# A two-layer transformer with routed experts on one core: bias in tiles on GpSimd, loads moved past returns, a count and a routing step moved, PSUM banks of the FFN reordered

## The chip, the cores and the metric

The kernel runs on one core of a Trainium2 chip. Its engines are TensorE (PE in the profile, PEld for its weight loads), VectorE (DVE), ScalarE (ACT), GpSimd (POOL) and SyncE (SP), which issues most transfers (DMA). The metric is the device time of one execution in microseconds (us); lower is better.

## The reference

Eight batches of 512 tokens by 512 features (fp32) pass through two layers. After each of the four blocks comes a layer norm over the features of block input plus block output.

```python
x = ln(x + attn0(x))   # 16 heads of 32, causal softmax, biases on q, k, v and the output
x = ln(x + ffn0(x))    # router: softmax over 8 experts, top 2; gated SiLU experts (512 -> 256 -> 512), with LoRA
x = ln(x + attn1(x))   # RMS-normed input, 8 query heads in 2 groups of 64, no mask, inner residual
x = ln(x + ffn1(x))    # 1408 hidden, integer weights minus 128, scaled by row, gated SiLU
```

## The kernel before

One program runs four stages, and TensorE is never meant to stop between them. A planner orders each engine's instructions when the program is built, from its own estimate of when each is ready; inside `in_order` the named engines keep the order of the source instead. Engines then run their lists in order and wait on semaphores. `tc.issue_after(i)` queues what is traced in it behind instruction i on i's engine, with no wait for i to finish; `add_manual_dep` with NoSync does the same for one pair on one engine.

*Attention of layer 0* (`attention0`, 0 to about 690 us). Eight batches b, four groups g of four heads, three units u of key tiles (`UNITS`: tile 0; tiles 1 and 3; tile 2). A unit computes scores (`scores`, PSUM tile sc), an exponential on ACT (L1476), a causal select on POOL for each key tile (`affine_select`, L1486), and, one unit later, the product with the values (`product`, av, L1503) and the sums on DVE (L1511). `normalise` takes the row sums (rs), a reciprocal (L1521), the product into aoT (L1522), and on POOL adds the inverses to g_total (L1077). The lists `todo[g, u]` hang other work between: q, k and v of this and the next batch, the output projection of the batch before (`project`, ps_o), its transposition, its router logits (`score`), and for the batch before that `choose` (top 2), `dispatch` (ranks) and `enter` (one-hot products into ps_table, read on DVE at L601 to L603). Batches 0 to 5 are transposed through DRAM (`Turn`: DVE blocks, four writes of 256 KB, one read back of 1 MB, L106), batches 6 and 7 by TensorE (`turn`, ps_x1T, L1427). The small PSUM tiles ps_q, ps_k, ps_o, ps_table, ps_count, ps_x1T and others take turns in the two banks of the pool "mm". Beside it POOL merges the LoRA deltas into the expert weights (L814, L823). In the loop over groups, g = 2 loads the next xT and adds the output bias to x on POOL (L1595, one instruction for the batch); g = 3 loads the next x. In the last batch `soon` counts the tokens of each expert (ps_count, L613 to L615) and takes the first rows to gather.

*Experts* (`Tiles`, to about 1061 us). Tiles of 128 tokens of one expert: gathered by POOL (`fetch`, L873, up to ten tiles ahead), transposed on DVE (`blocks`, L904), sent to DRAM and read back (pair, xrT), multiplied (`half` or `gate_up`, ps_gu), then `down` (ps_y), and written to results. One `step` does the half of tile i + 2 and the down of tile i. The first steps stand between the projection, turn, choose, dispatch and enter of the last batch. The tiles from number 16 on use tokens that `fixed` takes after the last enter.

*Attention of layer 1* (`Attention1`, to about 1607 us), all compute engines in order: `prepare` gathers two results a token (L722), adds and norms them, transposes through DRAM (`blocks`) or TensorE (`turn`). The rows of batches 2 to 7 (x, 1 MB each, L1969) are loaded ahead of it.

*FFN of layer 1* (`IntegerFfn`, to the end): `hidden` (ps_g, ps_u, L1222; ACT L1225; DVE L1227; then hT in a high and a low part) and `out` (ps_f, L1238). The last batch ends tile by tile in `last_rows`. PSUM has eight banks: in attention of layer 1 they go to "mm" (2), scores (2 tiles of 2 banks), av (2); the FFN pools d_gu (g and u, two each) and d_o (four) take all eight again.

Of the kernel before, what the change touches and what calls it, by code (L numbers as in the profile page):

```python
# [82 lines left out]
class Turn:  # L83
# [21 lines left out]
    def back(self, room):  # L105
        self.nc.sync.dma_start(out=room, in_=self.dram.rearrange("p k i f -> p (k i f)"))  # L106

# [319 lines left out]
class Router:  # L427
# [4 lines left out]
    def __init__(self, env, keep, pool, small, tmp, dram):  # L432
# [38 lines left out]
        nc.gpsimd.iota(i, pattern=[[0, 1]], base=0, channel_multiplier=1)  # L471
        lane = pool.tile([P, 1], F32, name="r_lane")
        nc.vector.tensor_copy(lane, i)
        self.signed = pool.tile([P, NT], F32, name="r_signed")
        for t in range(NT):
            nc.vector.tensor_scalar(self.signed[:, t : t + 1], lane, float(P * t - GAP + (P * t >= GAP)), None, ALU.add)
        i = tmp.tile([P, S], F32, tag="r_inv", name="r_columns_i", bufs=2)[:, : E * E_TILES].bitcast(I32)
        nc.gpsimd.iota(i, pattern=[[1, E * E_TILES]], base=0, channel_multiplier=0)
# [117 lines left out]
    def enter(self, ps, b, token, column, held, columns):  # L596

        nc, n = self.nc, TOP_K * NT
        for i in range(n):
            matmul_by_columns(nc, ps, token[:, i, :], column[:, i, :], i == 0, i == n - 1, columns)  # L600
        nc.vector.tensor_scalar(held, ps, 0.0, float((S + 1) * b + GAP), ALU.not_equal, ALU.mult)  # L601
        nc.vector.tensor_tensor(self.table, ps, self.table, ALU.add)
        nc.vector.tensor_tensor(self.table, held, self.table, ALU.add)  # L603

    def row_at(self, b, t):

        return (S + 1) * b + P * t + (P * t >= GAP)

    def soon(self, pool, ps, held):


        nc, half = self.nc, E // 2
        nc.tensor.matmul(ps, lhsT=self.ones, rhs=self.carry, start=True, stop=True)  # L613
        nc.vector.tensor_reduce(held, ps[:, :half], AX.X, ALU.min)
        nc.vector.tensor_scalar(held, held, float(SOON * P), None, ALU.is_ge)  # L615
        tokens = pool.tile([P, half, SOON], I32, name="t_soon")
        nc.vector.tensor_copy(tokens, self.by_expert()[:, :half, :SOON])
        return lambda e, j: tokens[:, e, j : j + 1]
# [9 lines left out]

    def tables(self, pool, ps, held):

# [7 lines left out]
        self.tokens = tokens = pool.tile([P, N_FREE + FREE], I32, name="t_tokens")  # L638
        nc.vector.memset(tokens, 0)
        nc.tensor.matmul(ps, lhsT=self.ones, rhs=self.carry, start=True, stop=True)  # L640
        n_i = pool.tile([P, E], I32, name="t_n_i")
        nc.vector.tensor_scalar(n_i, ps, P - 1.0, None, ALU.add)
# [184 lines left out]
class Tiles:  # L827
# [184 lines left out]

    def step(self):
        i = self.next
        self.next += 1
        if i == 0:
            self.down(i)
        if i + 2 < N_FIXED:
            self.half(i + 2)
        elif N_FIXED <= i + 1 < self.n:  # L1020
            self.gate_up(i + 1, lambda: self.turn_hidden(i))
        elif i + 1 == self.n:
            self.turn_hidden(i)
        while self.fetched <= i + 10 and (self.fetched < self.n_soon or self.of_fixed is not None):
            self.fetch(self.fetched)
            self.fetched += 1
        if i:
            self.down(i)
        for n in (4, 5) if i == 0 else (5,):
            if i + n < self.BY_BLOCKS:  # L1030
                self.turn_rows(i + n)
        if i + 6 >= self.BY_BLOCKS:
            self.pair_back(i + 6)
        if i + 7 >= self.BY_BLOCKS:
            self.blocks(i + 7)
# [109 lines left out]
class IntegerFfn:  # L1145
# [45 lines left out]
    def run(self, held_out, last_norm):  # L1191
        tc, nc, weights = self.env.tc, self.nc, self.weights
        with ExitStack() as phase:
            self.work = phase.enter_context(tc.tile_pool(name="d_work", bufs=1))
            self.p_gu = phase.enter_context(tc.tile_pool(name="d_gu", bufs=2, space=PSUM, reuse_waits="tile"))
            self.p_o = phase.enter_context(tc.tile_pool(name="d_o", bufs=1, space=PSUM, reuse_waits="tile"))
            weights.open(phase.enter_context(tc.tile_pool(name="d_weights", bufs=1)), 3 * NHID - weights.at)
            self.sd = self.work.tile([P, D], F32, name="sd")
            with tc.tile_pool(name="d_slots", bufs=1) as slots:
                while weights.at < 3 * NHID:  # L1200
                    weights.load(slots, 4, 3 * NHID)
                    weights.convert()
                nc.sync.dma_start(out=self.sd, in_=self.env.ins.s_down.partition_broadcast(P))
            with tc.tile_pool(name="d_raw", bufs=1) as self.raw:
                for b in range(NB - 1):
                    self.batch(b)
                    if b == 0:
                        last_norm()
                        ps = self.p_gu.tile([1, 1], F32, tag="g", name="ps_held")
                        nc.scalar.dma_start(out=held_out, in_=self.guard.partitions_held(self.env.const, ps))  # L1210
            self.late = phase.enter_context(tc.tile_pool(name="d_late", bufs=self.HELD))
            self.batch(NB - 1)
# [65 lines left out]
    def last_rows(self, b, t, x):  # L1278
# [8 lines left out]
        if t == NT - 1:  # L1287
            nc.vector.tensor_scalar(x, x, mv[:, 0:1], rstd, ALU.subtract, ALU.mult)
        else:
            shift = small.tile([P, 1], F32, name="shift2")  # L1290
            nc.gpsimd.tensor_scalar(shift, mv[:, 0:1], rstd, -1.0, ALU.mult, ALU.mult)
            nc.scalar.activation(x, x, AF.Identity, bias=shift, scale=rstd)
        nc.scalar.dma_start(out=env.ins.out[b][ts(t, P), :], in_=x)


def attention0(env, guard, keep, routes, experts, dram, p_mm, tiles_ctx):
# [8 lines left out]
    with ExitStack() as phase:  # L1305
# [102 lines left out]
        by_blocks = NB - 2  # L1408
        turns = Turn(env, dram, NT, "turned0")

        def room(b):
            x1Ts[b] = work.tile([P, ND, S], F32, tag="x1T", name="x1T")

        def blocks(b):
            room(b)
            flat = x1Ts[b].rearrange("p k s -> p (k s)")
            for t in range(NT):
                turns.blocks(flat, t, xs[b][:, t, :])
            turns.out(flat)
            turns.back(flat)  # L1420

# [36 lines left out]
        def enter(rows, mm=mm, columns=HD):  # L1458
            router.enter(mm([P, E * E_TILES], "ps_table"), *rows, columns)

        def scores(b, g, u):
# [22 lines left out]
            for kt in UNITS[u]:  # L1484
                first = p[:, :, at : at + P]
                nc.gpsimd.affine_select(out=first, in_=first, pattern=[[0, 4], [1, P]], compare_op=ALU.is_ge, fill=0.0,  # L1486
                                        base=0, channel_multiplier=-1)
                at += S - P * kt
            for thunk in merging.pop(n, []):
                thunk()  # L1490
# [23 lines left out]
        def normalise(b, g, acc):  # L1514
# [6 lines left out]
            nc.vector.reciprocal(r_inv, r_inv)  # L1521
            nc.vector.tensor_tensor(aoTs[b][:, g, :], av, r_inv, ALU.mult)  # L1522
            guard.watch_inverses(r_inv)

        merging = {}

        def plan(b):
# [26 lines left out]
            if b > 1:  # L1554
                todo[0, 0].append(lambda: choose(b - 2, mm=aside))
                todo[1, 0].append(lambda: dispatch(b - 2))
                todo[1, 2].append(lambda: enter(one_hot(b - 2, range(NT))))
            if last:
# [20 lines left out]
        def soon():  # L1579
            tiles.of_soon = router.soon(routes, mm([P, E], "ps_count"), guard.routed[:, 0:1])  # L1580

# [6 lines left out]
        for b in range(NB):  # L1588
            todo, late = plan(b)
            for g in range(ND):  # L1590
                if g == 2:
                    if b + 1 < NB:
                        load_xT(b + 1)

                    nc.gpsimd.tensor_tensor(xs[b], xs[b], row[:, 1:2, :].to_broadcast([P, NT, D]), ALU.add)  # L1595
                if g == 3 and b + 1 < NB:
                    load_x(b + 1)
                if b == NB // 2 and g == 0:
# [42 lines left out]
        score(b)  # L1641
        choose(b, P)
        tiles.step()
# [8 lines left out]
        order.close()  # L1652
    return router, tiles, router.tables(routes, p_mm.tile([P, E], F32, tag="mm", name="ps_count"), guard.routed[:, 1:2])


class Attention1:
# [21 lines left out]
    def prepare(self, b):  # L1678
# [17 lines left out]
        def blocks(t):  # L1696
# [3 lines left out]
            if t == NT - 1:  # L1700
                self.turn.out(st["room"])
                st["hT"] = own.tile([P, ND, S], F32, tag="hT", name="hT1")
                self.turn.back(st["hT"].rearrange("p k s -> p (k s)"))

# [62 lines left out]
    def batches(self, work, p_sc, p_av, weights, split):  # L1767
# [171 lines left out]
        prepare_table(AF.Silu)  # L1939
        banks += [p_sc.tile([P, 2, S], F32, tag="sc", name="ps_o1")[:, 0, :] for _ in range(2)]  # L1940
        banks.append(self.mm([P, D], "ps_o1"))
# [11 lines left out]
def usual_pass(tc, ins, held_out):  # L1953
    nc = tc.nc
    with ExitStack() as ctx:
# [4 lines left out]
        with tc.tile_pool(name="a_mm", bufs=2, space=PSUM) as p_mm, ExitStack() as attn1_ctx:  # L1960
# [28 lines left out]
            env.open_stream(ctx, range(2, NB), side="right")  # L1989
            for b in range(2, NB):  # L1990
                load_rows(b)
            weights = IntegerWeights(env, guard)
# [312 lines left out]
```

## Time and profile before

| | us |
|---|---|
| three runs: median (lowest to highest) | 2108.59 (2108.27 to 2109.18) |
| profiled execution | 2106.08 |
| its span, first to last instruction | 2104.20 |
| TensorE busy in the span | 2074.4 |
| first matmul starts / last matmul ends | 4.6 / 2095.2 |

Busy time adds up what an engine's instructions took; a matmul's end is modelled. A row of waits names who waited, on whom, for how long in total, how often, and the longest. A row of the timeline has start and length in us, then engine, line, operation, out<-in, and in brackets the idle time before it with what ended it. The granted TensorE clock was 0.999 on average.

### The profile page before, as it was taken

The numbers are of one execution on the slowest core, as the hardware profiler recorded it, in microseconds if no ns is written. First come the engines' busy times: TensorE is split into PE (matmuls) and PEld (weight loads), VectorE is DVE, ScalarE is ACT, GpSimd is POOL, SyncE is SP. The second block draws the span as 40 slices with busy tenths as digits, with TensorE's granted clock in tenths as the row PEclk, the third lists the DMA queues.
The fourth block names the chain that finished last, engine by engine and source line by source line (L and its number), as shares of the span: only waits on it lengthen the run. The fifth ranks groups of instructions, "written<-read, shape, count | busy, mean of one in ns | idle before, by whom it ended". The sixth has DMA issues, their size and how long they took to land. (4 is left out here: it accounts for less than half of the span.)

```text
span 2104.2 us, 35813 instructions
## 1 busy us (share of the span) xinstructions
PE 2074.4 (99%) x15074; PEld 1048.8 (50%) x15074; DVE 1270.6 (60%) x1963; ACT 606.8 (29%) x840; POOL 496.0 (24%) x488
## 2 busy tenths in 40 slices
PE   8999999999999999999999999999999999999998
PEld 2333333333334677774433333333335888888886
DVE  2666776776768623234257898887867644555443
ACT  2333433324333111111143333333332322222222
POOL 2343534434333221222042221223101000000000
PEclk9999999999999999999999999999999999999999
DMA  9020303415222568877451322132102311111000
GB/s 326 22 65 38 101 22 110 136 52 156 85 98 102 172 199 239 251 227 209 149 206 51 100 81 71 56 95 81 41 1 71 100 41 61 60 61 60 21 21 22
DMA packets 181946, 213.39 MB, mean 101 GB/s; under 512 B 72570, under 2 KB 125818, under 8 KB 178706
## 3 DMA queue, kind: packets, MB, share of 16 engines
q1 hardware_dynamic: 170496, 175.34, 26.8%
q0 software_dynamic: 10560, 34.61, 5.6%
q8 instruction: 121, 1.98, 0.4%
q10 hardware_dynamic: 722, 1.07, 0.1%
q14 instruction: 47, 0.39, 0.1%
HBM read 132.58 MB, written 78.40 MB: 100 GB/s over the span
## 5 line engine op out<-in xcount | busy, mean ns | idle before, releaser
L1077 POOL TENSOR_TENSOR g_total<-g_total,r_inv 128x512 f32<-128x512 f32 x64 | 90.1, 1408 | 488.3 <-DVE r_inv L1862 269.9
L1476 ACT ACTIVATE p<-sc 128x2048 f32<-128x2048 f32 (+1 forms) x96 | 153.0, 1594 | 174.7 <-PE sc L65 150.7
L1511 DVE TENSOR_TENSOR p<-p 128x1536 f32<-128x1536 f32 (+2 forms) x96 | 149.5, 1557 | 77.6 <-POOL p L1486 74.4
L1227 DVE SCALAR_TENSOR_TENSOR hT<-ps_u,vec,sg 128x512 f32<-128x512 f32 x88 | 65.6, 745 | 187.2 <-PE ps_u L1222 187.1
L1238 PE MATMUL ps_f<-ffn_w,h_half 128*128 128x512 f32 x664 | 168.1, 393 | 2.6 <-DVE h_half L1233 2.0
L958 PE MATMUL ps_gu<-xrT,experts 128*128 128x256 f32 x736 | 166.7, 380 | 0.4 <-DMA xrT<-pair 0.4
L958 PEld LDWEIGHTS ps_gu<-xrT,experts 128*128 128x128 f32 x736 | 139.5, 190 | 35.6 <-issue 19.2
L1832 ACT ACTIVATE p<-sc 128x1024 f32<-128x1024 f32 x128 | 124.2, 1022 | 100.2 <-PE sc L65 91.5
L1862 DVE RECIPROCAL r_inv<-r_inv 128x512 f32<-128x512 f32 x32 | 107.1, 3346 | 67.8 <-ACT r_inv L1074 67.8
L1238 PEld LDWEIGHTS ps_f<-ffn_w,h_half 128*128 128x128 f32 x664 | 122.9, 188 | 34.6 <-DVE h_half L1233 8.0
L1222 PE MATMUL ps_g<-x_high,ffn_w 128*128 128x512 f32 x352 | 137.3, 390 | 0.9 <-DVE x L1804 0.9
L1222 PE MATMUL ps_g<-x_low,ffn_w 128*128 128x512 f32 x352 | 137.2, 390 | 0.0
L1222 PE MATMUL ps_u<-x_low,ffn_w 128*128 128x512 f32 x352 | 137.1, 390 | 0.0
L1222 PE MATMUL ps_u<-x_high,ffn_w 128*128 128x512 f32 x352 | 137.1, 389 | 0.0
L65 PE MATMUL sc<-qT,kT 64*64 64x512 f32 x1024 | 124.7, 602 | 1.2 <-ACT qT L1729 0.9
L65 PE MATMUL ps_q<-experts 128*32 128x512 f32 x1024 | 120.8, 601 | 4.9 <-DMA experts<-in_xT 4.6
L65 PE MATMUL ps_v<-experts 128*32 128x512 f32 x1024 | 120.9, 595 | 0.0
L1851 PE MATMUL av<-p,v 128*64 128x512 f32 x512 | 120.9, 594 | 0.0
L1486 POOL TENSOR_SCALAR_AFFINE_SELECT p<-p 128x512 f32<-128x512 f32 x128 | 82.7, 657 | 157.6 <-ACT p L1476 155.0
L1225 ACT ACTIVATE sg<-ps_g,vec 128x512 f32<-128x512 f32 x88 | 60.6, 689 | 199.8 <-PE ps_g L1222 199.8
L65 PE MATMUL ps_o<-attn_out,aoT 128*64 128x512 f32 x512 | 116.4, 598 | 0.0
L65 PE MATMUL ps_k<-experts 128*32 128x512 f32 x1024 | 116.3, 595 | 0.0
(278 smaller groups left out, 3248.3 us busy)
## 6 DMA issues: line engine op xcount, KB each, us to landing
results<-y SPq DMA_DIRECT2D x68, 256.0 KB, 3.2
pair<-xrT SPq DMA_DIRECT2D x30, 512.0 KB, 3.0
xrT<-pair SPq DMA_DIRECT2D x120, 128.0 KB, 3.8
turned<-turned SPq DMA_DIRECT2D x56, 256.0 KB, 4.0
x<-in_x SPq DMA_DIRECT2D x8, 1024.0 KB, 8.6
rows<-x SPq DMA_DIRECT2D x32, 256.0 KB, 2.3
x<-rows SPq DMA_DIRECT2D x16, 512.0 KB, 12.5
experts<-in_xT SPq DMA_DIRECT2D x7, 1024.0 KB, 8.5
```

Source lines behind the costliest of these rows:

```text
L65: nc.tensor.matmul(out[m], lhsT=lhsT[:, m], rhs=rhs, start=start, stop=stop)
L958: nc.tensor.matmul(ps[:, j, :], lhsT=w, rhs=xT[:, c, :], start=c == 0, stop=c == ND - 1)
L1077: self.nc.gpsimd.tensor_tensor(self.total, self.total, r_inv, ALU.add)
L1222: nc.tensor.matmul(ps, lhsT=w[:, ts(dc, P)], rhs=x[:, dc, :], start=(dc, i) == (0, 0), stop=(dc, i) == (ND - 1, 1))
L1227: nc.vector.scalar_tensor_tensor(hT, u, vec[:, V_SU + c : V_SU + c + 1], sg, ALU.mult, ALU.mult)
L1238: self.nc.tensor.matmul(os[t], lhsT=h[:, ts(t, P)], rhs=self.weights(2 * NHID + c), start=(c, i) == (0, 0), stop=(c, i) == (NHID - 1, 1))
L1476: nc.scalar.activation(p, sc[:, :, :width], AF.Exp, scale=scale)
L1486: nc.gpsimd.affine_select(out=first, in_=first, pattern=[[0, 4], [1, P]], compare_op=ALU.is_ge, fill=0.0, base=0, channel_multiplier=-1)
L1511: nc.vector.tensor_tensor(total[:, :, P * kt :], total[:, :, P * kt :], p[:, :, at : at + w], ALU.add)
L1832: nc.scalar.activation(p, sc, AF.Exp, scale=scale)
L1851: nc.tensor.matmul(st["av"][HD * j : HD * (j + 1), :], lhsT=st["v"][:, kt, HD * j : HD * (j + 1)], rhs=p[:, j, :], start=kt == 0, stop=kt ...
L1862: nc.vector.reciprocal(r_inv, r_inv)
```

## The change

1. The bias of layer 0 is no longer added for a whole batch at g = 2. Batches 1 to 6 add tile 0, tiles 1 and 2, and tile 3 behind the selects of unit 1 in groups 1, 2 and 3; batch 7 adds two tiles in group 1 and two in group 2; batch 0 keeps one add, behind the selects of group 2.
2. From batch 1 on xT of the next batch is loaded at g = 0, and x of the next batch is queued behind the read back of the turned rows (`returned`).
3. `soon` only copies the carry; the count, its minimum and its comparison go to `tables`. In the last batch the product of L1522 is queued behind `enter`'s read of the table (`behind`).
4. In the last batch `choose` goes into a step (`amid`, between its half and its down), and with this one more step stands before `dispatch` and all that follows it.
5. d_o is opened before d_gu; two output tiles of attention of layer 1 use the second half of their score buffers.
6. Only the rows of batch 2 are loaded ahead of layer 1's attention; those of batch b + 1 are queued behind the read back of batch b.
7. The last tile of the output is normed and written in two halves, from two queues.

```diff
+        self.soon_carry = pool.tile([P, half], F32, name="r_soon_carry")
+        nc.vector.tensor_copy(self.soon_carry, self.carry[:, :half])
-        nc.tensor.matmul(ps, lhsT=self.ones, rhs=self.carry, start=True, stop=True)
-        nc.vector.tensor_reduce(held, ps[:, :half], AX.X, ALU.min)
-        nc.vector.tensor_scalar(held, held, float(SOON * P), None, ALU.is_ge)
...
         nc.tensor.matmul(ps, lhsT=self.ones, rhs=self.carry, start=True, stop=True)
+        nc.tensor.matmul(soon, lhsT=self.ones, rhs=self.soon_carry, start=True, stop=True)
+        nc.vector.tensor_reduce(held_soon, soon, AX.X, ALU.min)
+        nc.vector.tensor_scalar(held_soon, held_soon, float(SOON * P), None, ALU.is_ge)
...
-    def step(self):
+    def step(self, amid=lambda: None):
...
+        amid()
         if i:
             self.down(i)
...
+            self.p_o = phase.enter_context(tc.tile_pool(name="d_o", bufs=1, space=PSUM, reuse_waits="tile"))
             self.p_gu = phase.enter_context(tc.tile_pool(name="d_gu", bufs=2, space=PSUM, reuse_waits="tile"))
-            self.p_o = phase.enter_context(tc.tile_pool(name="d_o", bufs=1, space=PSUM, reuse_waits="tile"))
...
-            nc.vector.tensor_scalar(x, x, mv[:, 0:1], rstd, ALU.subtract, ALU.mult)
+            for i, queue in enumerate((nc.sync, nc.scalar)):
+                half = x[:, ts(i, D // 2)]
+                nc.vector.tensor_scalar(half, half, mv[:, 0:1], rstd, ALU.subtract, ALU.mult)
+                queue.dma_start(out=env.ins.out[b][ts(t, P), ts(i, D // 2)], in_=half)
...
+            if u == 1 and b:
+                with tc.issue_after(select.ins):
+                    for t in ((), (0, 1), (2, 3), ())[g] if b == NB - 1 else ((), (0,), (1, 2), (3,))[g]:
+                        x = xs[b][:, t, :]
+                        nc.gpsimd.tensor_tensor(x, x, row[:, 1, :], ALU.add)
+            elif (g, u) == (2, 1):
+                with tc.issue_after(select.ins):
+                    nc.gpsimd.tensor_tensor(xs[b], xs[b], row[:, 1:2, :].to_broadcast([P, NT, D]), ALU.add)
...
-                todo[1, 2].append(lambda: enter(one_hot(b - 2, range(NT))))
+                if last:
+                    todo[1, 2].append(lambda: behind(enter(one_hot(b - 2, range(NT))), normed[0]))
+                else:
+                    todo[1, 2].append(lambda: enter(one_hot(b - 2, range(NT))))
...
-                if g == 2:
-                    if b + 1 < NB:
-                        load_xT(b + 1)
-
-                    nc.gpsimd.tensor_tensor(xs[b], xs[b], row[:, 1:2, :].to_broadcast([P, NT, D]), ALU.add)
+                if g == (0 if b else 2) and b + 1 < NB:
+                    load_xT(b + 1)
                 if g == 3 and b + 1 < NB:
-                    load_x(b + 1)
+                    with tc.issue_after(returned[0].ins) if b else ExitStack():
+                        load_x(b + 1)
...
-        choose(b, P)
+        tiles.step(lambda: choose(b, P))
         tiles.step()
         dispatch(b, tiles.bank, P)
...
-                self.turn.back(st["hT"].rearrange("p k s -> p (k s)"))
+                back = self.turn.back(st["hT"].rearrange("p k s -> p (k s)"))
+                if 2 <= b < NB - 1:
+                    with self.env.tc.issue_after(back.ins):
+                        self.load_rows(b + 1)
...
-        banks += [p_sc.tile([P, 2, S], F32, tag="sc", name="ps_o1")[:, 0, :] for _ in range(2)]
+        banks += [p_sc.tile([P, 2, S], F32, tag="sc", name="ps_o1")[:, 1, :] for _ in range(2)]
...
-            for b in range(2, NB):
-                load_rows(b)
+            load_rows(2)
+            attention.load_rows = load_rows
```

Beside these, the small tile r_lane shares a buffer with r_columns.

## The prediction

> **What bounds the kernel now.** I read the page's first part, then TensorE's own waits, then the timeline and the transfers around each wait.
>
> ```profile
> PE 2074.4 (99%) x15074; PEld 1048.8 (50%) x15074; DVE 1270.6 (60%) x1963; ACT 606.8 (29%) x840; POOL 496.0 (24%) x488
> ```
>
> TensorE is busy for 2074.4 of 2104.2 us, and the change removes no matmul, so only the other 29.8 us can be won. Its first matmul starts at 4.6 us and its last ends at 2095.2 us: 4.6 us lie ahead, 9.0 us behind, some 16.2 us between. TensorE's waits name those (what waited, on whom: total, times, longest):
>
> ```profile
> PE ps_q L65 <- DMA experts<-in_xT: 4.6, 1, 4.6
> PE ps_f L1238 <- DVE h_half L1233: 2.0, 7, 0.5
> PE av L1503 <- POOL p L1486: 1.9, 3, 1.0
> PE ps_logits L504 <- DMA x1T<-turned: 1.8, 2, 1.5
> PE ps_x1T L1427 <- DVE g_routed L614: 1.5, 1, 1.5
> PE sc L65 <- ACT p L1476: 1.2, 1, 1.2
> PE sc L65 <- ACT qT L1729: 0.9, 1, 0.9
> PE ps_g L1222 <- DVE x L1804: 0.9, 1, 0.9
> ...
> PE ps_r L65 <- ACT logits L1440: 0.8, 1, 0.8
> PE ps_rank L65 <- DVE earlier L553: 0.7, 1, 0.7
> PE ps_f L1238 <- issue: 0.6, 1, 0.6
> PE rs L1518 <- ACT first_turned L925: 0.6, 1, 0.6
> ...
> PE ps_gu L958 <- DMA xrT<-pair: 0.4, 1, 0.4
> ```
>
> Rows 3, 4, 5, 8 and the ps_r and ps_rank rows are what the edits touch: 1.9 + 1.8 + 1.5 + 0.9 + 0.8 + 0.7 = 7.6 us. All other work runs beside TensorE, so an edit counts only through such a row, or through a new one.
>
> **The change part by part.** Signs: minus is time won.
>
> *Bias on POOL, -1.9 us.* Before, one add for a whole batch:
>
> ```profile
> L1595 POOL TENSOR_TENSOR x<-x,row 128x2048 f32<-128x2048 f32 x8 | 36.5, 4560 | 9.3 <-DMA x<-in_x 3.7 <-DMA results<-g_total 3.3 <-issue 2.3
> ```
>
> The planner put it where x lands, in group 3 of the batch before. At 498.21 and 583.68 it stands ahead of two selects whose exponential ended at 497.51 and 582.57; the selects start at 502.73 and 588.19, and av waits 0.60 and 1.01 us (0.27 in the batch at 158.7). After, each piece is queued behind the select pair of unit 1. A 128x512 add on POOL took 1.27 us at best (L823 at 469.63) and 1.77 on average (L823 and L814), so 28 pieces are 36 to 50 us plus 4.56 for batch 0: up to 18 us more POOL work, on an engine busy 24%. What waits behind a piece: the add of g_total, a merge, the next select. In groups 1 and 2 the pair ended at 457.43 and POOL was idle for 10.1 us; two slow pieces (4.5 us at the 2.26 of the slower merges) fit. In group 3 the pair would end near 498.9 and the next exponential ends at 502.95: 4 us for one piece. The last batch has two pieces behind the selects that end at 656.32, and the next select is ready at 660.65; two gathers of first rows move back by 2 to 4 us, of which none feeds the two tiles turned at 669. I take the whole row; the ends are -1.9 and rival B.
>
> *Loads apart from returns, -1.8 us.* Both waits on x1T are for the 1 MB return of the transposed rows. Around the longer one, by the transfers from 400 to 420 us (KB, us to landing):
>
> ```profile
> x<-in_x SPq DMA_DIRECT2D x1, 1024.0 KB, 8.4
> x1T<-turned SPq DMA_DIRECT2D x1, 1024.0 KB, 8.6
> ```
>
> x was issued at 404.07 and landed at 412.51; the return, issued at 408.74, landed at 417.39, 4.9 us after x; TensorE wanted it at 416.07. The four writes ahead, issued from 400.10 on, landed at 408.62 with x behind them. Now x is issued behind the return, and the next xT at the start of the batch, some 60 us earlier. The Trainium skill (DMA: Bandwidth & Descriptors, "Queues, rings and completion order") says that SP's descriptors start in ring order on each DMA engine but that completion is not first in, first out. Read as order, the return needs only its 4.9 us: landing at 413.6, 2.5 us to spare, -1.8. Read as sharing, x issued 0.4 us behind takes its half again and the sum here is 0. The 4.9 us after x's landing speak for order; I take -1.8. SP's queue: six xT loads move ahead of rows, merges and turns of their batch. A merge load behind one would wait up to 8.4 us more; the loads issued at 430.02 and 431.09 are used at 445.36, 12 us after landing. x is next used by the bias, 30 us or more later. Both are costed at nothing because of these leads; without them a late merge add would hold the select behind it, as the 4.56 us add did.
>
> *The count moved, and an order edge, -1.2 us.* The timeline of the last batch (start, us):
>
> ```profile
> 647.04 0.68 DVE L1522 TENSOR_TENSOR aoT<-av,r_inv 128x512 f32<-128x512 f32 x1
> 648.24 0.41 DVE L601 TENSOR_SCALAR one_hot<-ps_table 128x256 f32<-128x256 f32 x1
> 648.58 0.41 DVE L602 TENSOR_TENSOR r_table<-ps_table,r_table 128x256 f32<-128x256 f32 x1
> 648.90 0.15 DVE L614 TENSOR_REDUCE g_routed<-ps_count 128x1 f32<-128x4 f32 x1
> 649.13 1.06 PE L1427 MATMUL ps_x1T<-ident,x 128*128 128x128 f32 x8 [1.46 <-DVE g_routed L614]
> ```
>
> The two "mm" banks go round: ps_k, ps_table, ps_count, first ps_x1T, second ps_x1T. The first ps_x1T takes ps_table's bank, read until 648.98, so dropping L614 alone would win 0.1. But without ps_count it takes ps_k's bank, read by ACT at 644.61: it starts at 647.67. The second now takes ps_table's, wanted near 648.2. The edge puts L1522 (0.68) behind L602, so that read ends near 648.3. Left: 0.1 to 0.4 of 1.46; I take -1.2. Only the release of an av bank waits for L1522, needed again about 10 us later. Added: a 128x4 copy (0.17, the row of L551); count, reduce and compare (0.3) move to the table stage, where TensorE is busy 303.56 of 304 us and DVE 93.
>
> *Routing moved, -1.5 us.* ps_r waited 0.76 for the logits copy, ps_rank 0.72 for choose's chain on DVE (724.67 to 730.91). In between now stand a half (3.6 us) before ps_r, and a down (1.9), another half and a down (5.5) before ps_rank: 7.4 against 6.2. Both rows go. But gathers of fixed rows, first at 744.21, start one step (5.3 us) later against the tiles. Their transposes already wait on DVE (2.2 and 0.8 us), without holding TensorE. The pair that came 0.44 late at 758 shared its return (8 us instead of 3 to 5) with these gathers and gains. I take -0.2 for it; ends -0.4 and +5.3 (rival C).
>
> *FFN banks, -0.6 us.* The first ps_g waits 0.85 for the last residual (1607.24 to 1607.98), which reads its bank. By the order of the pools ps_g now gets the unread half of a score buffer. Next in line is ps_f at 1616.21, 0.62 late: hT ran at 1614.71, behind two norms and a weight conversion on DVE, although its inputs were there at 1611.97. If that order stays, the 0.85 only moves into this wait: 0. If the planner puts hT first, both go: -1.5. I take -0.6.
>
> *Rows of layer 1, -0.3 us.* Twelve 512 KB loads stood beside the gathers at 1068 to 1078, which took 7.9 us each against 3.5 to 5 at 1119 to 1129. Now two do. POOL's sums start 3.6 us sooner; TensorE's small waits on that chain up to 1107 add to 0.9, of which some belongs to bank turns. Ends 0 and -0.9. The later loads, one batch at a time, have 40 us.
>
> *Last tile in halves, -0.4 us.* L1288 took 0.55, its transfer 2.5 to landing. The first half leaves 0.25 sooner, each carries half. The same page ("Rules for kernel authors") speaks against this: spreading transfers over issuing engines doesn't help, they share the same DMA engines[...]. In the trace the bytes move in about 1 us of the 2.5, so at most 0.5 and the 0.25. Between: -0.4, ends 0 and -0.6.
>
> *Restarts, -0.6 us.* A wait costs more than its idle time: at 1616.21 matmuls start 1.01 apart instead of 0.23, 0.78 for 0.62 idle. Nine waits by 0.16 are 1.4; I take 0.6, since most stand before short or column-tiled matmuls.
>
> Sum: 1.9 + 1.8 + 1.2 + 1.5 + 0.2 + 0.6 + 0.3 + 0.4 + 0.6 = 8.5. The planner reorders every engine after such edits; for new waits I give back 1.0. So -7.5 us: the profiled execution from 2106.08 (span 2104.20 plus 1.88) to 2098.6; its before stands 2.5 under the median of 2108.59, so the median goes to 2101.1.
>
> **The rivals.** *A: the waits move.* The next name in each queue takes over: hT in the FFN, the table's read, x beside the return. For: those three are within 1 us of the waits removed. Against: margins of 2.5 and 4 us elsewhere. Gain 3: 2105.6. This also holds the case that an edge changes nothing.
>
> *B: slower, through POOL's pieces.* Instead of one add a batch, 20 groups have a piece in front of the next select. If each holds av by 0.63 (the mean of the three waits), that is 12.6, against 8.5 - 1.9 - 1.0 = 5.6 of other gains: +7, 2115.6. It decides when a piece and the g_total add outlast 4 us in group 3, or 10 us in groups 1 and 2. Against: the slowest such adds took 2.3.
>
> *C: fixed rows late.* One step once, 5.3: gain 2 left, 2106.6.
>
> **How the numbers follow.** Measured runs spread by 0.04%; 0.2%, 4.2 us, is about what can be told from no change. Forecast 0.64, all faster; A 0.20 (0.02 faster, 0.16 same, 0.02 slower); C 0.05 (0.04 same, 0.01 slower); B 0.11. So 0.66, 0.20, 0.14. With every part at its better end the sum is 12: 2096.5. The forecast's own range is 2096.5 to 2104.3; to 2109 it takes in A and C, leaving out B and a tail.
>
> **What would show it.** Right: no av row on POOL L1486, no ps_logits row on x1T, under 0.4 us before ps_x1T, no ps_r and ps_rank rows, ps_g without a wait, gathers near 5 us in layer 1's first batch, TensorE busy the same 2074. Wrong: a ps_f wait grown to 1.4 us (FFN part 0); av waits in groups 1 to 3 (B); ps_gu waiting on xrT between 760 and 800 us (C); a return still landing 8 us after its issue.

## The result: 0.9% slower, and the profile after

| | before | after |
|---|---|---|
| median of six runs, us (lowest to highest) | 2108.89 (2107.06 to 2111.30) | 2127.34 (2125.17 to 2130.59) |
| profiled execution / its span, us | 2106.08 / 2104.20 | 2128.18 / 2126.2 |
| mean granted TensorE clock | 0.999 | 0.995 |

The ratio is 1.0087 (95% interval 1.0074 to 1.0100): slower by 18 us, where 7.5 us of gain were forecast, and outside the range. The page's row of TensorE and its waits after the change, in the order that they were shown of before:

```profile
PE 2081.2 (98%) x15074; PEld 1049.7 (49%) x15074; DVE 1286.7 (61%) x1965; ACT 607.2 (29%) x840; POOL 502.2 (24%) x509
```

```profile
PE ps_logits L505 <- DMA x1T<-turned: 12.3, 4, 5.5
PE av L1522 <- POOL p L1497: 5.8, 6, 1.0
PE ps_q L65 <- DMA experts<-in_xT: 4.6, 1, 4.6
PE rs L1887 <- DVE total L1868: 3.1, 1, 3.1
...
PE ps_f L1245 <- PE ps_u L1229: 0.8, 1, 0.8
PE ps_x1T L1438 <- DVE r_table L603: 0.7, 1, 0.7
PE ps_rank L65 <- DVE earlier L554: 0.7, 1, 0.7
```

Read the rows against the list that the prediction gave itself. The rows of ps_g, ps_r and ps_gu are gone, and ps_x1T halved. But the return of the turned rows, which was to vanish (1.8), became the largest wait of all; av, which was to vanish (1.9), waits 5.8; and rs, 0.2 before, waits 3.1. Up to its last matmul TensorE was idle for 35.9 us instead of 20.8: 15.1 more. And it was busy for 6.8 us more (2081.2 against 2074.4) with the same 15074 matmuls: that is the clock, worked out below. The two make the 22 us between the spans.

**The return.** SP's own timeline in batch 4 shows what stands ahead of the read back of the turned rows (start, length, queue, line). Before, and then after:

```profile
404.07 1.24 SPq L1330 DMA_DIRECT2D x<-in_x  x1
408.74 0.33 SPq L106 DMA_DIRECT2D x1T<-turned  x1
409.11 2.00 SPq L824 DMA_DIRECT2D merged<-merged  x2
411.16 1.34 SPq L1326 DMA_DIRECT2D experts<-in_xT  x1
```

```profile
414.25 2.61 SPq L830 DMA_DIRECT2D merged<-merged  x2
416.95 0.42 SPq L1336 DMA_DIRECT2D experts<-in_xT  x1
417.55 0.43 SPq L106 DMA_DIRECT2D x1T<-turned  x1
418.02 0.43 SPq L1340 DMA_DIRECT2D x<-in_x  x1
```

Now x is behind the return as the edge says, and the planner has filled the place ahead of it with xT, which is as large (1024 KB). In both lists it is the xT of two batches on (batch 6): before the change, too, the planner issued it a batch ahead of the source line that loads it. Two merged stores, which wait for POOL's merges, stand ahead as well, and the return is issued 3.5 us before TensorE wants it (417.55 for 421.06) where it was 7.3 before (408.74 for 416.07). It lands 8.9 us after its issue (8.6 before), and TensorE waits 5.5.

**The pieces.** All six av waits are alike, 0.97 us in group 3 of batches 1 to 6, behind two pieces in group 2. The groups of VectorE by form show which neighbour changed, the norm L195 of 128x512 (busy, mean ns). Before, and then after:

```profile
L195 DVE TENSOR_SCALAR x<-x,mv,rstd 128x512 f32<-128x512 f32 x60 | 33.3, 616 | 15.5 <-POOL rstd L193 15.5
```

```profile
L195 DVE TENSOR_SCALAR x<-x,mv,rstd 128x512 f32<-128x512 f32 x60 | 44.9, 810 | 15.5 <-POOL rstd L193 15.5
```

In batch 4 the two pieces and the four norms run side by side:

```profile
400.27 2.86 POOL L1504 TENSOR_TENSOR x<-x,row 128x512 f32<-128x512 f32 x2
398.96 4.46 DVE L195 TENSOR_SCALAR x<-x,mv,rstd 128x512 f32<-128x512 f32 x4 [1.48 <-POOL rstd L193]
```

The group took 11.6 us more for six batches of two pieces, which is 0.97 us of VectorE for each piece beside it. The pieces pay as well: 1.44 to 1.46 us each there, 1.27 to 1.30 elsewhere. In batch 4 the four norms took 4.46 us instead of 2.53; the transposes, the reciprocal, the g_total add on POOL and the select behind that add came later in turn, and av waited for the select.

### The profile page after: what moved, and what is told of

It reads as the page before. It is cut to its first block, busy times and chain, and to the rows that moved or that the text cites. A ratio compares the mean times of both kernels' runs of the same rounds, so it can differ in the third digit from the quotient of the medians.

```text
span 2126.2 us, 35858 instructions
## 1 busy us (share of the span) xinstructions
PE 2081.2 (98%) x15074; PEld 1049.7 (49%) x15074; DVE 1286.7 (61%) x1965; ACT 607.2 (29%) x840; POOL 502.2 (24%) x509
## 4 chain that ended last, share of the span: by engine, by line
PE 43%; DVE 4%; issue 1%; DMA 1%; POOL 1%; ACT 0%; DVEq 0%; POOLq 0%; ACTq 0%
PE ps_f L1245 6%; PE ps_u L1229 6%; PE ps_g L1229 6%; PE sc L65 5%; PE ps_o L65 5%; PE av L1879 5%; PE ps_q L65 5%; PE rs L1887 1%; PE ps_v L65 1%; PE ps_k L65 1%; DVE y_ffn L1251 1%; DVE x L195 1%; DVE x L1252 1%; DVE stats L190 1%; DMA yr<-results,r_results_i 0%
## 5 line engine op out<-in xcount | busy, mean ns | idle before, releaser
L964 PEld LDWEIGHTS ps_gu<-xrT,experts 128*128 128x128 f32 x736 | 139.3, 190 | 35.9 <-issue 19.2
L65 PE MATMUL ps_q<-hT,attn_qkv 128*64 128x512 f32 (+1 forms) x504 | 116.4, 597 | 0.0
## 6 DMA issues: line engine op xcount, KB each, us to landing
x<-in_x SPq DMA_DIRECT2D x8, 1024.0 KB, 10.3
```

The source lines that it names most:

```text
L65: nc.tensor.matmul(out[m], lhsT=lhsT[:, m], rhs=rhs, start=start, stop=stop)
L964: nc.tensor.matmul(ps[:, j, :], lhsT=w, rhs=xT[:, c, :], start=c == 0, stop=c == ND - 1)
```

## The experiments

Each kernel was timed beside the kernel before, on the same chip. The medians of before were 2106.6, 2106.2 and 2106.0 us in the three groups of runs, so kernels of different groups are compared by their ratio to before.

| run | median, us | ratio to before (95%) |
|---|---|---|
| changed kernel | 2127.34 | 1.0087 (1.0074 to 1.0100) |
| e1 xT behind the return too | 2115.06 | 1.0036 (1.0023 to 1.0050) |
| e2 x ahead again | 2110.41 | 1.0021 (1.0014 to 1.0028) |
| e3 one add again | 2153.27 | 1.0222 (1.0208 to 1.0235) |
| e4 rows first again | 2123.20 | 1.0080 (1.0066 to 1.0094) |
| f1 = e2, no piece in group 2 | 2105.99 | 0.9998 (0.9990 to 1.0006) |
| f2 = f1, rows first | 2104.77 | 0.9992 (0.9984 to 1.0001) |
| f3 count, routing, banks, last tile alone | 2104.81 | 0.9991 (0.9983 to 1.0000) |
| f4 pieces alone | 2111.22 | 1.0027 (1.0018 to 1.0037) |
| g1 = f2, pieces in groups 0, 1, 3, 3 | 2100.39 | 0.9976 (0.9968 to 0.9985) |
| g2 = f2, one piece in each group | 2103.95 | 0.9989 (0.9981 to 0.9997) |
| g3 = g1, rows as changed, output weights later | 2101.05 | 0.9976 (0.9968 to 0.9984) |

### e1: xT behind the return as well

```diff
                 if g == (0 if b else 2) and b + 1 < NB:
-                    load_xT(b + 1)
+                    with tc.issue_after(returned[0].ins) if returned[0] else ExitStack():
+                        load_xT(b + 1)
```

> The changed kernel, in which the load of xT too is queued behind the return of the turned rows (x already is); nothing else. Theory Q (place in SP's queue): the changed kernel waits 12.3 us for returns because xT, 1 MB, took the place ahead of the return that x had before, with two merged stores ahead of it. With neither load ahead, the return lands about 5 us after its issue as the one of batch 6 did (5.4): the waits of 5.5 and 4.6 us fall to under 1 us each, batch 6 keeps its 1.6, the ps_logits row comes to 2 to 3 us, and the stretches of half clock behind the two long waits go: 10 us of idle time and 4 to 6 us of slow matmuls, so 2111 to 2114. Rival S (sharing): whatever is issued around the return takes its half of the 16 engines, ahead or behind: the returns still take 8 us or more and the time stays above 2120.

From 1.0087 to 1.0036: some 11 us faster than the changed kernel, where 13 to 16 were expected. TensorE's waits for the return:

```profile
PE ps_logits L505 <- ACT p L1487: 2.5, 2, 1.2
...
PE ps_logits L505 <- DMA x1T<-turned: 1.9, 1, 1.9
```

In batch 4 the return was issued at 416.67, x 0.4 and xT 1.4 us behind it, and the matmul that needs it started at 421.91: 5.2 us at most, with 2 MB queued right behind. (The row that names ACT ends with that matmul too; what ACT did had long been done.) So what stands behind a return does not slow it, what stands ahead does: Q holds and S falls. 4.4 us of waits are left. The merged stores are still ahead of the return here; in e2, where they stand behind it, these waits are gone.

### e2: x ahead again

```diff
-                    with tc.issue_after(returned[0].ins) if b else ExitStack():
-                        load_x(b + 1)
+                    load_x(b + 1)
```

> The changed kernel with one line undone: x of the next batch is no longer queued behind the return. Theory Q: x goes back to its place ahead of the return and xT behind, as before; the return is issued 3 us sooner in batches 4 and 5 (no merged stores ahead), the ps_logits row falls from 12.3 to about 1.8 us, half clock goes after the two long waits: 2110 to 2114. If instead xT's move to the start of the batch did the harm, xT still stands ahead of the return and the row stays above 8 us: above 2122.

```profile
PE av L1522 <- POOL p L1497: 5.9, 6, 1.0
PE ps_q L65 <- DMA experts<-in_xT: 4.4, 1, 4.4
PE rs L1886 <- DVE total L1867: 2.9, 1, 2.9
...
PE ps_logits L505 <- DMA x1T<-turned: 0.5, 1, 0.5
```

One line undone takes the ratio from 1.0087 to 1.0021, 14 us, and the return's row to 0.5. SP's list is again x, return, merged stores, xT, although xT is still called at g = 0. So the earlier call of xT by itself moves nothing; it was x's edge that moved xT up. The edge without the earlier call was not run.

### e3: one add for a batch, as before

```diff
-            if u == 1 and b:
-                with tc.issue_after(select.ins):
...
+                if g == 2:
+                    nc.gpsimd.tensor_tensor(xs[b], xs[b], row[:, 1:2, :].to_broadcast([P, NT, D]), ALU.add)
```

> The changed kernel with the bias as before, one add of 128x2048 for a batch, free of any order edge. Theory D (the pieces behind the selects of group 2 run beside the norm on DVE and slow it, 4.46 us in place of 2.53 for the four L195): the norm takes 2.5 us again, the six waits of 0.97 of av on the select of group 3 go (5.8 us in all), and the old waits of about 1.9 us on the 4.56 us add come back: 3 to 4 us faster than the changed kernel, 2123 to 2125. Rival P (a piece holds the next select in POOL's queue): the waits go too, but the norm was slow for another reason and stays at 4.4 us.

A clear miss, since 3 to 4 us of gain were expected: 28 us slower than the changed kernel by the ratios (1.0222 against 1.0087). The norm did take 2.5 us again, so far D held. But POOL's timeline in the batch at 350 shows what the expectation left out:

```profile
354.41 4.49 POOL L1613 TENSOR_TENSOR x<-x,row 128x2048 f32<-128x2048 f32 x1 [9.30 <-DMA x<-in_x]
358.86 1.23 POOL L1497 TENSOR_SCALAR_AFFINE_SELECT p<-p 128x512 f32<-128x512 f32 x2
```

The planner placed the add too early for this x. With x behind the return, POOL stands 9.3 us in front of the add, waiting for x, and the selects stand behind it; TensorE waits 8.7 us for them here, 28.9 in four such places. So with x's edge the bias has to be tied to a late place: the change's first two parts hang together, and the prediction costed them apart. In f3, which has the one add but x ahead, the av row is 3.9.

### e4: the rows of layer 1 first

```diff
-            load_rows(2)
-            attention.load_rows = load_rows
+            for b in range(2, NB):
+                load_rows(b)
```

> The changed kernel with the rows of batches 2 to 7 all loaded ahead of layer 1's attention, as before. Theory R: with the rows gone, weight loads of attention and FFN had moved up beside the first gathers, and the gathers took 8 to 11 us, the row sums' total came 3.1 us late and half clock followed. With the rows back the gathers take 7.6 to 8.8 us, the rs wait falls from 3.1 to 0.2 us, half clock behind it goes: about 2.9 + 1.7 = 4.6 us faster, 2122 to 2124. Rival: the late total has nothing to do with the rows; then the wait stays near 3 us and the time at 2127.

The rs wait of 3.1 us is gone from the waits, and the sum that needs the second gather starts 9.4 us after the stage's first load instead of 12.6 (9.7 before). But the ratio only moves from 1.0087 to 1.0080, 1.5 us where 4.6 were expected, and the intervals overlap. The trace shows 3 us of waiting gone and a stretch of half clock with it; the times do not settle how much of that lasts.

### f1: no piece beside the norm

```diff
-                    for t in ((), (0, 1), (2, 3), ())[g] if b == NB - 1 else ((), (0,), (1, 2), (3,))[g]:
+                    for t in ((), (0, 1), (2, 3), ())[g] if b == NB - 1 else ((), (0, 1), (), (2, 3))[g]:
```

> The kernel of e2 (x ahead of the return again) with the pieces of batches 1 to 6 moved: two behind the selects of group 1, none in group 2, two in group 3. Theory D: the two pieces of group 2 ran beside the norm L195 on VectorE and stretched it from 2.53 to 4.46 us; through the transposes and the reciprocal the g_total add and the select behind it came 1.9 us late. With none there the norm takes 2.5 us, the six av waits (5.8 us) go and nothing comes in their place, since POOL has 10 us behind the selects of group 1: e2 minus 5.8, about 2104.6. Rival P (a piece behind a pair of selects costs in POOL's queue wherever it stands): two pieces in groups 1 and 3 hold the next select there: waits of about 1 us appear in those groups, and the time stays at 2109 to 2111, or grows.

By the ratios f1 is 4.8 us below e2, where 5.8 were expected. The six av waits are gone and L195 is back at 617 ns. Yet a new row stands in their place, as P had it, for D's reason:

```profile
PE rs L1537 <- DVE q L1394: 2.8, 5, 0.6
```

```profile
372.79 0.70 DVE L593 TENSOR_SCALAR one_hot<-r_columns,r_to_column 128x256 bf16<-128x256 bf16 x1
373.41 1.30 DVE L592 TENSOR_SCALAR one_hot<-r_columns,to_lane,r_signed 128x128 bf16<-128x128 bf16 x1
374.63 1.35 DVE L593 TENSOR_SCALAR one_hot<-r_columns,r_to_column 128x256 bf16<-128x256 bf16 x1
375.90 0.30 DVE L592 TENSOR_SCALAR one_hot<-r_columns,to_lane,r_signed 128x128 bf16<-128x128 bf16 x1
```

POOL's two pieces ran from 373.38 to 375.89. Just then two VectorE instructions of 0.3 us took 1.3 each; at 375.90 all is normal. Each piece holds one instruction for about 1.0 us, here too, and q behind the one-hots comes late.

### f2: rows first as well

The edit is f1's and e4's together.

> The kernel of f1 with the rows of batches 2 to 7 loaded ahead of layer 1's attention, as before the change. If the three causes are separate and add up (x's edge, pieces beside the norm, weight loads beside the first gathers), the rs wait of 2.9 us falls to 0.2: f1 minus 2.7, about 2101.9, that is 4 to 5 us faster than the kernel before. If they don't add up, some other wait takes the place, and it stays at 2104 or above.

The rs wait on the total is gone, but f2 is only 1.2 us below f1 by the medians where 2.7 were expected, with overlapping intervals. f1's row of 2.8 us for q stays, so the absolute time missed, and in the same stage a wait has come that no expectation had:

```profile
PE sc L65 <- issue: 1.4, 1, 1.4
```

It ends at 1077.29: TensorE waits for the copy of qT on ACT, which started 2.5 us after its ps_q was done (0.05 in the kernel before). The trace ties this delay to no instruction of the core, so its cause is open. The wait is there, 1.4 to 1.5 us long, in f2, f3, f4, g1, g2 and g3, and not in the other seven traces.

### f3: the rest of the change alone

Bias, loads of x and xT and layer 1's rows as before; count, routing, banks and last tile as changed.

> The changed kernel with bias, loads of x and xT, and layer 1's rows as before: what is left is the count and its edge, the routing step, the FFN banks and the last tile in halves. From the changed kernel's waits: ps_x1T 1.46 to 0.74, ps_r 0.76 and ps_gu 0.44 gone, ps_g 0.85 gone against 0.16 more at ps_f, and 0 to 0.4 at the end: 2.6 to 3.0 us faster than the kernel before, 2103.6 to 2104.0. Rival: these edits reorder engines elsewhere and their waits come back: within 1 us of the kernel before.

1.4 us faster by the medians, where 2.6 to 3.0 were expected, with an interval that just reaches 1. The rows that were to shrink did, 2.6 us in sum; 2.0 of it went to the av row, which is 3.9 in five waits here against 1.9 in three before: the one add meets other selects. Two more rows moved though nothing here aimed at them: the new wait of 1.4 for qT, and the return's 1.8 of before, which is gone with the loads in their old order. So that row differs from trace to trace by as much as the prediction hoped to win from it.

### f4: the pieces alone

The edit is that part of the change, on the kernel before.

> The kernel before with the bias alone in pieces, as the change places them. Theory D: six av waits of 0.97 us in group 3 come (5.8), the three old ones go (1.9): 3.9 us slower than the kernel before, 2110.5. Rival: the waits need the moved loads as well (x late beside the norm): no new waits, 1 to 2 us faster than before.

```profile
PE av L1511 <- POOL p L1486: 5.8, 6, 1.0
```

5.0 us slower by the medians (3.9 expected), with L195 at 810 ns and x loaded as before: D, without any help from the loads.

### g1: pieces where VectorE has time

```diff
-                    for t in ((), (0, 1), (2, 3), ())[g] if b == NB - 1 else ((), (0, 1), (), (2, 3))[g]:
+                    for t in ((), (0, 1), (2, 3), ())[g] if b == NB - 1 else ((0,), (1,), (), (2, 3))[g]:
```

> The kernel of f2 with one of the two pieces of group 1 moved to group 0 (batches 1 to 6: one in group 0, one in group 1, none in 2, two in 3). In f1 and f2 a piece of 1.27 us on POOL stretched the bf16 one-hot products beside it on DVE (L592, L593) from 0.3 to 1.3 us: about 1.0 us of DVE time for one piece, so two of them in group 1 made q (L1394) 2 us late and rs waited 5 times 0.55. Theory D (what a piece costs is the DVE work it runs beside): with one piece in group 1 the five rs waits go, as they weren't there in e2; in group 0 DVE has 1.85 us idle before q, so one piece there costs nothing: f2 minus 2.8, about 2102. Rival: a piece costs wherever it stands, a wait of about 0.5 comes in group 0: 2104 to 2105.

No av row, no row of q, no row of the return is left among the waits (rs on the total is 0.8); 5.6 us faster than before by the medians, and 1.6 better than the 2102 expected. This is the version that beats both: x ahead of the return, pieces in groups 0, 1 and 3, rows first. POOL does as much bias work as in the changed kernel; only its neighbours differ.

### g2: one piece in each group

```diff
-                    for t in ((), (0, 1), (2, 3), ())[g] if b == NB - 1 else ((), (0, 1), (), (2, 3))[g]:
+                    for t in ((), (0, 1), (2, 3), ())[g] if b == NB - 1 else ((0,), (1,), (2,), (3,))[g]:
```

> The same with one piece behind the selects of each of the groups 0 to 3, so that one (not two, not none) stands beside the norm L195 in group 2. Theory D in numbers: two pieces made the chain behind the norm 1.9 us late and cost 0.97 each time, so its slack is about 0.95; one piece makes it 0.97 late, so the av waits are 0 to 0.2 us each: 2102 to 2103. If a piece blocks for its whole place in POOL's queue whatever the number, waits of 0.5 us or more stay six times: 2105 or more.

The norm in group 2, with one piece beside it, by VectorE's groups:

```profile
L195 DVE TENSOR_SCALAR x<-x,mv,rstd 128x512 f32<-128x512 f32 x60 | 39.1, 714 | 15.5 <-POOL rstd L193 15.5
```

617, 714 and 810 ns with none, one and two pieces: 0.97 us for each piece, on a line. No av wait is left, as the slack of 0.95 said. The total missed by 1 us, and the return's row is 3.0 (2.1 in batch 4). The norm, 0.97 later, sends the turned rows later, a second user that the expectation had not counted. That is not the whole of it: in e2 the rows are as late against TensorE, and in batch 4 nothing waits, since there the return was issued 7.9 us after the first write and landed within 7.3; here it was 8.6 and 8.7. What makes this difference between traces, no run shows.

### g3: output weights after the gathers

```diff
-        for j in range(2):
-            nc.sync.dma_start(out=w_out[HD * j : HD * (j + 1), :, :],
...
+        def load_out():
+            for j in range(2):
+                nc.scalar.dma_start(out=w_out[HD * j : HD * (j + 1), :, :],
...
+                todo[6].append(load_out)
```

> The kernel of g1 with layer 1's rows one batch at a time, as the change has them, but the two loads of the output weights (64 partitions, 512 KB each, L1805) issued by ACT in the seventh step of the first batch, past the gathers, instead of by SP right behind the rows. Theory R1 (these loads, 13.9 us long, are what holds the gathers at 8 to 11 us): the gathers take 4 to 7 us, the rs wait is under 0.3 us, and the time is that of g1 or up to 1 us less. Rival R2 (any traffic there does, the ffn_i load of 512 KB is still beside them): gathers stay above 8 us and the rs wait above 2 us: g1 plus 2.5.

The rs wait is 1.0, against 1.9 to 3.1 in the five kernels that have the rows as changed and the weights early, and the second gather's sum starts 9.9 us after the stage's first load (12.6 in the changed kernel), with the ffn_i load still beside it. That speaks for R1: in this trace the output weights carry most of the delay. It is not the whole of it: 0.3 was expected, and g1, with the rows first and the weights far behind, has a wait of 0.8 and that sum at 11.7, where f2, whose loads stand the same here, has none and 10.3. Between traces with the same loads these times differ by 1 to 2 us. In time g3 equals g1, so the times show no gain from it.

## Why the prediction was wrong

*Loads apart from returns (-1.8): the step "the next xT at the start of the batch, some 60 us earlier" failed.* The choice of order over sharing was right: e1's return, with 2 MB behind it, took 5.2 us, near the 4.9 assumed. But xT was not issued 60 us earlier. The planner already had the xT of batch 6 at 411.16, in batch 4, ahead of either source line, so the earlier call moved nothing (e2), and the edge on x freed a place ahead of the return that xT took. "SP's queue: costed at nothing" named the queue and not that place. Price by e2: 14 us. The 1.8 to be won was not firm either (f3).

*Bias (-1.9): the step that costed a piece by its place in POOL's queue failed.* The 28 pieces took 37.5 us, within the 36 to 50 given, and POOL had the room. What they cost is VectorE's time, 0.97 us a piece. f4: 5.0 us slower. Rival B named the place, group 3's select behind the g_total add, at over twice the price (12.6 for the 5.8 measured) and by another mechanism, a piece in POOL's own queue. The Trainium skill (SBUF — State Buffer, "Who interferes with whom") has a rule that fits: VectorE and GpSimd share a pair of ports as an exclusive lock, and tensor_scalar in its two-port modes takes it, while tensor_tensor on GpSimd reads through it. In which mode the norms ran the trace does not say; that each side slows the other it does. By the rule each piece would hold VectorE for its whole 1.45; measured are 0.97. Weighed then, against the norm that stands beside the selects of group 2, two pieces of 1.27 would have been 2.5 us of delay, an estimate by that page, where the slack was about 1 (1.93 us of delay made a wait of 0.97).

*The clock: not in the sum at all.* 6.8 us of TensorE's busy time. "Restarts" allowed at most 0.16 us for a wait, and waits of 5 us were not foreseen.

*Rows (-0.3): the step "gathers near 5 us" failed.* The eight gathers took 8.1 to 10.7 us instead of 7.6 to 8.8. Taking 5 MB away from them only let the next loads of SP's list move up beside them, and by g3's trace the output weights are worse company. The sign was wrong; the price is 1.5 us by e4's ratio, 3 by the wait in the trace and up to 1.7 for the clock behind it.

*Count and edge (-1.2):* the right mechanism, 0.7 (ps_x1T 1.46 to 0.74). *Routing (-1.5 and -0.2):* ps_r went (0.76), ps_gu went (0.44), ps_rank stayed at 0.7. The step that failed there is "7.4 against 6.2": choose's chain took 8.0 us after (747.45 to 755.42), with three instructions of 0.7 us for expert tiles (L966, and L910 twice) between its last steps on VectorE. *FFN banks (-0.6):* 0.7, since ps_g's 0.85 went and ps_f's 0.62 became 0.78. The planner did put hT first, as the better end asked, and ps_f came no sooner after ps_g (8.3 us, 8.2 before), now behind a weight conversion on VectorE that ended at 1638.18. So the number came out near by luck. *Last tile (-0.4):* nothing; from the last matmul to the end it took 9.1 us after, 9.0 before. *Fixed rows (rival C):* no wait of ps_gu on xrT came. So four small parts stood at 3.9 together and gave 2.6 by their rows; the two large ones had the wrong sign. *Giving back (1.0)* was sized for reorderings under a microsecond and met one of 14. Taken singly, x's edge (14), the pieces (5.0, f4), the rows (1.5) and the four small parts (-1.4, f3) make 19 us against the 18 measured.

## What to carry to other kernels

An order edge on one transfer says nothing of what takes its place: before costing a load at nothing, ask which ready load the planner will put ahead of the one that matters, and tie that too, or leave the order alone. Work on GpSimd has a second price, the VectorE instructions that it runs beside; it is cheap only where VectorE has slack, and moving a piece by one group was worth 3 to 4 us here. A wait on TensorE that fills over half of a 3.4 us window costs more than itself.

## What the runs showed of the hardware

*The clock falls in windows.* In all thirteen traces the granted clock changes at times that lie a whole number of 3.413 us apart. Below, in windows laid on that grid, stand length, TensorE's busy time, granted clock and DMA share; first batch 4 of the changed kernel:

```profile
418.73:422.14 3.41, 2.33 (x44) 1.00 1.00 317
422.14:425.55 3.41, 0.00 (x0) 1.00 0.99 401
425.55:428.97 3.42, 2.38 (x16) 0.50 0.93 332
428.97:432.38 3.41, 3.41 (x26) 0.50 0.07 24
432.38:435.79 3.41, 3.41 (x44) 1.00 0.72 204
```

The window without work is followed by two at half clock: 5.79 us of busy time in them at half speed, some 2.9 lost besides the 5.5 of the wait. In the three such stretches, two of 6.8 us and one of 3.4, TensorE was busy for 14.3 us, of which half, 7.1, is an estimate of the loss; 6.8 more were measured than before, which has no such stretch. For f1, e4, e1 and e3, which have such stretches too, the same sum gives 3.1, 4.2, 4.8 and 13.8, where 3.0, 3.7, 4.8 and 12.8 us more than before were measured. The six timed executions of the changed kernel all had a mean granted clock of 0.993 to 0.996, so the loss is not the profiled one's alone. A short wait can be enough. Here are e1 in batch 6 and then the changed kernel in batch 6:

```profile
592.92:596.34 3.42, 1.57 (x41) 1.00 0.95 355
596.34:599.75 3.41, 3.41 (x26) 0.50 0.83 298
```

```profile
606.47:609.88 3.41, 1.81 (x40) 1.00 0.97 366
609.88:613.30 3.42, 3.42 (x46) 1.00 0.71 253
```

1.57 us busy, 46% of the window, and the clock halves; 53%, and it does not. Over all thirteen traces, from the clock's first record (near 10 us) to the last matmul, each of the 23 windows with over half its length idle (54% at least, from full clock) was followed by half clock, and of the windows at full clock with less (up to 49% idle) none. The wait of 2.9 us in e2 lay across the border of two windows, 49% and 37% idle, and cost nothing more. The Trainium skill (TensorE: Matmul & The Clock Gate, "Part 1: The HAM clock gate") knows the free-running window of 3413 ns and puts the fall after an idle window; here a window 54% idle was enough.

*GpSimd beside VectorE:* each 128x512 add of GpSimd's cost VectorE's tensor_scalar beside it about 1.0 us, fp32 norms (g2: 0.97) and bf16 one-hots (f1: 0.3 became 1.3) alike.
